# Three of four time norms move from token rows to token columns, with their statistics sent as rows through DRAM; the v mix of the first block waits for the r mix

## The chip, the core and the metric

The kernel runs on one core of one Trainium2 chip. A core has five engines with queues of their own: TensorE (PE, with its weight loads listed as PEld), VectorE (DVE), ScalarE (ACT), GpSimd (POOL) and SyncE (SP, which here only issues transfers). Each engine runs its instructions in the order of its queue; an instruction that waits holds up everything behind it on the same engine. ACT, POOL and SP also issue DMA transfers, and a transfer that waits holds up its queue in the same way. The metric is the device time of one execution in microseconds (us).

## The reference

The input x has 2048 tokens of 512 channels, all float32. The kernel computes an RWKV layer on the layer norm of x, adds x, and then adds a gated feed-forward layer on the layer norm of that sum. Cut to the part that matters here:

```python
xn = layernorm(x)                       # no gain or bias
h  = layer_norm(xn, ln1_g, ln1_b)       # a second norm with gain and bias
hh = time_shift(h)                      # h of the token before
k  = (h*tm_mk + hh*(1-tm_mk)) @ Wk.T
v  = (h*tm_mv + hh*(1-tm_mv)) @ Wv.T
r  = (h*tm_mr + hh*(1-tm_mr)) @ Wr.T
x1 = xn + (sigmoid(r) * wkv(k, v)) @ Wo.T
h2 = layer_norm(x1, ln2_g, ln2_b)       # mixed again, then Wkey, Wval and Wcr
...                                     # then x + that, one more norm, gate, up, down
```

The mean and variance of a norm are taken over the 512 channels of one token. The gain, the bias and the mix factors belong to channels. The matrix products sum over channels.

## The kernel before, in words

The tokens are cut into NB = 4 blocks of TB = 512. Each block has two layouts. With **tokens on partitions**, a tile is 128 tokens by 4 x 512 elements; a mean or a scale is then one number per partition. With **channels on partitions**, a tile holds 4 chunks of 128 channels by 512 tokens; gain, bias and mix factors are then one number per partition, and the products can use the tile as it is. TensorE has to go from the first layout to the second by transposes, 16 of 128x128 for each norm of a block.

The first norm of a block is `time_norm` (L753). It takes the moments of x (`moments`, L396: BATCH_NORM_STATS2 and AGGREGATE, L399 and L400), from them two scales per token (`rsqrt`, L405: for block 1 one GpSimd power at L409, for blocks 2 and 3 three Newton steps on VectorE), scales and centres x into `h` on VectorE (`scaled`, L424, four instructions at L389), and calls `shifted_norm` (L448). That transposes h on TensorE (`transposed`, L436, the matmuls at L441) and lets ScalarE apply gain and bias while it reads PSUM (L453, tile `hT_a`). Block 0 has its own form, `first_block` (L772), with transposes at L810. The residual tile x1 is made on ScalarE from the loaded x and the first of the two scales (L742).

From `hT_a` come three mixed operands, for k, r and v (`mix`, L484): for each chunk of channels one ScalarE multiplication (`shifted`, L494) and one VectorE multiply-add (`mixed`, L393). Where an operand is used by a fast matrix scheme with seven products, four differences (`sums_of`, L462) follow. The second norm, `channel_norm` (L933), has the same shape and fills `hT_b`, from which come the operands `cr` (for `gate_unit`, L951) and `ck` (for `up_unit`, L959). In the second half of the kernel `ffn_in` (L1001) transposes once more.

**What sets the order.** The orders on TensorE, VectorE and ScalarE are fixed by hand: the program is recorded in one pass, and each of those engines keeps the order of recording. The products are laid down one by one (`unit`, L537: seven products; `plain_unit`, L632: the ordinary scheme). After each product of four matmul calls the recorder calls `tick` (L293), which fills an estimated budget of other work (`STEP` = 1.72, charged by `cost`, L204) from queues of generators: `hot`, then `background` (L227 takes the first hot item and the first three background items in turn). `yield 1` in a generator means "let the next item go on"; `need` (L318) forces an item to its end when a product is about to want it. So more VectorE work in one generator moves what comes behind it to later ticks, until `need` forces it. A mix is put into the background by `push_mix` (L862), with a condition: the norm must be finished and an operand tile free.

TensorE has six PSUM banks from one pool (`bank`, L102) and two fixed ones. Weights come by SP through a ring of 12 tiles of 256 KB (`wring`, L77). The tiles of 1 MB for whole blocks of tokens come from a pool of five (`tokp`, L79). GpSimd loads weights, VectorE forms differences of their quarters, and GpSimd stores these to DRAM for later (`prepare`, L144), all through the first half.

Of the kernel before, what the change touches and what calls it, by code (L numbers as in the profile page):

```python
# [9 lines left out]
F32 = mybir.dt.float32  # L10
AF = mybir.ActivationFunctionType
ALU = mybir.AluOpType
# [3 lines left out]
P = 128  # L16
H = 512
NC = H // P
TB = 512
NT = TB // P  # L20
# [9 lines left out]
LN1G, LN1B, LN2G, LN2B, FIRST, MK, MV, MR, CK, CR = range(10)  # L30
NVEC = 10

WK, WV, WR, WO, WCR = range(5)

PLAIN = {(0, WK), (0, WR), (0, WV), (0, WO), (1, WK), (1, WR)}
WKEY = 5
WVAL = 9
# [23 lines left out]
def rwkv_ffn_kernel(  # L61
    ctx: ExitStack,
    tc: tile.TileContext,
    x: bass.AP,
    vecs: bass.AP,
    w: bass.AP,
    wd: bass.AP,
# [2 lines left out]
    nc = tc.nc  # L70
    ntok = x.shape[0]
    NB = ntok // TB
# [12 lines left out]
    dram = ctx.enter_context(tc.tile_pool(name="dram", bufs=1, space=bass.MemoryType.DRAM))  # L85
# [3 lines left out]
    htp = mixes.enter_context(tc.tile_pool(name="htp", bufs=2))  # L89
# [9 lines left out]
    def tok_tile(name):  # L99
        return tokp.tile([P, NT, H], F32, tag="tok", name=name)  # L100
# [103 lines left out]
    def cost(n, fixed=0.135, per=0.00107):  # L204
        spent[0] += max(0.17, fixed + per * n)
# [7 lines left out]
    def flush():  # L213
        while put_off:
            flush_one()
# [27 lines left out]
    finished = set()  # L243
# [68 lines left out]
    def push(name, gen, ready=None):  # L312
        background.append([ready, gen, name, False, background])
# [18 lines left out]
    ident = const.tile([P, P], F32, name="ident")  # L332
# [6 lines left out]
    pt = ps.tile([P, 2, HB], F32, tag="ps", name="warm")  # L339
# [27 lines left out]
    carry = {}  # L367
# [4 lines left out]
    def vcol(row, c):  # L372
        return vec[:, row, c : c + 1]
# [22 lines left out]
    def moments(src, mv):  # L396
        for t in range(src.shape[1]):
            st = small.tile([P, 6], F32, tag="st", name="st")
            nc.vector.bn_stats(st, src[:, t, :])  # L399
            nc.vector.bn_aggr(mv[:, t, :], st)  # L400
            cost(512)
            cost(0)
            yield
# [32 lines left out]
    def transposed(h, evacuate):  # L436
        for c in range(NC):
            pt = bank()
            flat = pt.rearrange("p a b -> p (a b)")
            for t in range(NT):  # L440
                nc.tensor.transpose(  # L441
                    flat[:, t * P : (t + 1) * P], h[:, t, c * P : (c + 1) * P], ident
                )
            evacuate(c, flat)
            spent[0] += 0.4
            yield

    def shifted_norm(s, h, hT, g, b):  # L448
        nc.vector.tensor_copy(hT[:, :, 0:1], carry[s])
        cost(0)  # L450

        def evacuate(c, pt):
            nc.scalar.activation(  # L453
                hT[:, c, 1:], pt, AF.Identity, bias=vcol(b, c), scale=vcol(g, c)
            )

        yield from transposed(h, evacuate)
        yield 1
        nc.vector.tensor_copy(carry[s], hT[:, :, TB : TB + 1])
        cost(0)  # L460
# [11 lines left out]
    def op_free():  # L472
        return live_ops[0] < 3
# [236 lines left out]
    def product_of(b, n, name, sink, by_token, done=None, free=op_done):  # L710
        if (b, name) not in ops:
            flush()
        plain = (b, n) in PLAIN
        B = Lazy((b, name), plain)
# [18 lines left out]
    x1s, ops, hTs = {}, {}, {}  # L733
# [12 lines left out]
    def affine(var, mv):  # L746


        n = mv.shape[1]
        ts(var[:, :n], mv[:, :, 1], EPS, None, ALU.add)  # L750
        ts(var[:, n : 2 * n], mv[:, :, 1], 1.0 + EPS, EPS * EPS, ALU.mult, ALU.add)

    def time_norm(b):  # L753
        xb = xin.pop(b)
        mv = small.tile([P, NT, 2], F32, tag="mv", name="mv")
        yield from moments(xb, mv)
        var = small.tile([P, 2 * NT], F32, tag="var2", name="var2")
        affine(var, mv)
        two = small.tile([P, 2 * NT], F32, tag="two", name="two")
        yield from rsqrt(var, two, 2 * NT, b == 1)  # L760
        rstd, both = two[:, :NT], two[:, NT:]
        h = tok_tile("h")
        yield from scaled(xb, h, mv, both)
        hT = htp.tile([P, NC, TB + 1], F32, tag="hT", name="hT_a")
        hTs[b, "a"] = hT
        tails[b] = residual(b, xb, [(mv[:, t, 0:1], rstd[:, t : t + 1]) for t in range(NT)])
        if b == 1:
            yield 1
        yield 1
        yield from shifted_norm("a", h, hT, LN1G, LN1B)  # L770

    def first_block():  # L772

# [76 lines left out]
    tails = {}  # L850
# [7 lines left out]
    def time_mix(b, name):  # L858
        row, n = {"k": (MK, WK), "r": (MR, WR), "v": (MV, WV)}[name]
        yield from mix((b, name), hTs[b, "a"], row, (b, n) in PLAIN)  # L860

    def push_mix(b, name, gen):  # L862
        norm = f"normb{b}" if name in ("cr", "ck") else f"norm{b}"
        push((b, name, "t"), gen, lambda: norm in finished and op_free())

    qs = {}

# [38 lines left out]
    def v_unit(b):  # L906
# [5 lines left out]
        def done():  # L912
            hidden_sums((b, "g"), q, (b, WO) in PLAIN)

# [367 lines left out]
    for n in "rv":  # L1282
        push_mix(0, n, time_mix(0, n))
# [77 lines left out]
def _layout(inputs):  # L1361

    import numpy as np

    def get(name):
        return np.asarray(inputs["L0_" + name])

    x = np.ascontiguousarray(get("attn_x").reshape(-1, H))
    names = ["ln1_g", "ln1_b", "ln2_g", "ln2_b", "tm_first", "tm_mk", "tm_mv", "tm_mr", "cm_mk", "cm_mr"]
    vecs = np.stack([get("attn_" + n).reshape(NC, P).T for n in names], axis=1)  # L1370

    gu = get("ffn_w_gate_up")
    half = gu.shape[0] // 2
    gate, up = gu[:half], gu[half:]
    key, val, down = get("attn_Wkey"), get("attn_Wval"), get("ffn_w_down")
    blocks = [get("attn_" + n) for n in ("Wk", "Wv", "Wr", "Wo", "Wcr")]
    blocks += [key[j * H : (j + 1) * H] for j in range(4)]
    blocks += [val[:, j * H : (j + 1) * H] for j in range(4)]
    blocks += [gate[j * H : (j + 1) * H] for j in range(4)]
    blocks += [up[j * H : (j + 1) * H] for j in range(4)]  # L1380

    def quarter(m, i, j):
        q = m[i * HB : (i + 1) * HB, j * HB : (j + 1) * HB]

        return q.T.reshape(2, P, HB).transpose(1, 0, 2)

    w = np.stack(
        [
            np.stack([quarter(m, i, j) for i, j in ((0, 0), (0, 1), (1, 1), (1, 0))])
            for m in blocks  # L1390
        ]
    )
    def quarter_quarter(i, j, m, k):
        at = slice(i * HB + m * P, i * HB + (m + 1) * P)
        lo = j * HB + k * P

        q = [down[at, g * H + lo : g * H + lo + P].T for g in range(4)]
        return np.stack(q, axis=1).reshape(P, 4 * P)

    places = ((0, 0), (0, 1), (1, 1), (1, 0))  # L1400
    wd = np.stack(
        [np.stack([quarter_quarter(i, j, m, k) for m, k in places]) for i, j in places]
    )
    return {
        "x": x,
        "vecs": np.ascontiguousarray(vecs),
        "w": np.ascontiguousarray(w),
        "wd": np.ascontiguousarray(wd),
    }
# [19 lines left out]
```

## Time and profile before

| what | value |
|---|---|
| median of 3 runs (lowest to highest) | 1241.83 us (1241.83 to 1243.77) |
| the profiled execution: its time, its span | 1242.04 us, 1239.9 us |
| PE busy | 1231.2 us, 99% |
| DVE busy | 704.8 us, 57% |
| ACT busy | 356.9 us, 29% |
| POOL busy | 153.7 us, 12% |
| transferred | 290.12 MB, mean 234 GB/s |
| transposes L441: for hT_a and hT_b (112), for z (64) | 14.2 us, 7.6 us busy |
| scaling h from x and the two scales (L389, 16) | 8.1 us, 542 ns each |
| hT_a from PSUM (L453, 12) | 8.6 us, 779 ns each |

A line of the groups names the source line, the engine, the operation, the tile written and the tiles read, the shapes, the count, the busy time, the mean duration of one, and the idle time of the engine before them with what ended it. In the timeline a line begins with its start and its length. The chain is read back from the last instruction: at each step to what released it. A matmul call of 128x256 in float32 is two MATMUL records; a transpose is one.

### The profile page before, as it was taken

The page shows a single profiled execution, that of the slowest core. Times are in us where ns is not written, and L with a number is a line of the kernel's source. Part 1 is how long each engine was busy: PE and PEld are TensorE (multiplying, and loading weights), DVE is VectorE, ACT ScalarE, POOL GpSimd, SP SyncE. Part 2 cuts the span into 40 slices and gives each one's busy share as a digit, 9 for nine tenths or more (in the row PEclk, how much of TensorE's full clock was granted, in tenths as well). Part 3 has the DMA queues.
Part 4 walks back from the last instruction along what each step waited for, and adds up shares of the span by engine and source line. Part 5 has one row for each costly group of instructions (what it writes and reads, how often), then busy time and mean ns, then how long its engine had stood idle before and what let it go on. Part 6 is the DMA issues. An engine that isn't in the chain of part 4 may idle for free.

```text
span 1239.9 us, 18124 instructions
## 1 busy us (share of the span) xinstructions
PE 1231.2 (99%) x6552; PEld 1105.0 (89%) x6552; DVE 704.8 (57%) x1307; ACT 356.9 (29%) x661; POOL 153.7 (12%) x278
## 2 busy tenths in 40 slices
PE   8999999999999999999999999999999999999998
PEld 7888888888888888888888888998899888998898
DVE  5877686487763758523542365556546365462466
ACT  5534352142631334212311232122221222112211
POOL 2232221222212222221100000000000000000000
PEclk9999999999999999999999999999999999999999
DMA  6768885898778887899756755895569845785576
GB/s 204 238 216 286 288 277 199 295 318 288 247 255 261 283 261 240 262 329 305 229 145 181 225 144 151 268 339 153 145 183 302 275 141 154 240 295 160 152 223 204
DMA packets 138983, 290.12 MB, mean 234 GB/s; under 512 B 17424, under 2 KB 18576, under 8 KB 137872
## 3 DMA queue, kind: packets, MB, share of 16 engines
q1 hardware_dynamic: 116448, 217.11, 57.4%
q0 software_dynamic: 21440, 70.27, 15.5%
q10 hardware_dynamic: 1008, 1.59, 0.3%
q8 instruction: 53, 0.87, 0.3%
q14 instruction: 34, 0.28, 0.1%
HBM read 246.96 MB, written 41.94 MB: 233 GB/s over the span
## 4 chain that ended last, share of the span: by engine, by line
PE 96%; ACT 1%; DVE 1%; DMA 1%; POOL 0%; issue 0%; DVEq 0%
PE ps L556 54%; PE ps L1160 14%; PE accv L556 11%; PE accx L556 11%; PE ps L658 6%; PE ps L441 1%; DMA raw<-in_wd 1%; ACT mix L494 0%; DMA x<-in_x 0%; ACT mix L823 0%; ACT hT_a L815 0%; DVE mix L393 0%; DVE resid L385 0%; DVE r L385 0%; POOL raw L149 0%
## 5 line engine op out<-in xcount | busy, mean ns | idle before, releaser
L556 PE MATMUL ps<-zT,w 128*128 128x256 f32 x1280 | 289.5, 379 | 0.0
L556 PEld LDWEIGHTS ps<-zT,w 128*128 128x128 f32 x1280 | 241.9, 190 | 32.2
L556 PE MATMUL ps<-mix,w 128*128 128x256 f32 x920 | 210.8, 379 | 0.2 <-ACT u L587 0.2
L556 PEld LDWEIGHTS ps<-mix,w 128*128 128x128 f32 x920 | 174.5, 190 | 24.2 <-ACT u L587 0.6
L385 DVE TENSOR_TENSOR u<-u,accx 128x512 f32<-128x512 f32 x66 | 45.2, 684 | 119.8 <-ACT accx L591 119.8
L1160 PE MATMUL ps<-w,hid 128*128 128x128 f32 x832 | 104.5, 275 | 0.0
L556 PE MATMUL ps<-w,t 128*128 128x256 f32 x456 | 102.3, 379 | 0.0
L1160 PEld LDWEIGHTS ps<-w,hid 128*128 128x128 f32 x832 | 99.8, 192 | 0.8
L556 PEld LDWEIGHTS ps<-w,t 128*128 128x128 f32 x456 | 86.4, 190 | 11.6
L1160 PE MATMUL ps<-w,quads 128*128 128x128 f32 x704 | 89.0, 275 | 0.4 <-ACT r L1172 0.4
L576 ACT COPY accv<-ps 128x512 f32<-128x512 f32 x66 | 37.6, 570 | 179.3 <-PE ps L556 179.3
L1160 PEld LDWEIGHTS ps<-w,quads 128*128 128x128 f32 x704 | 84.2, 192 | 0.9 <-ACT r L1172 0.5
L385 DVE TENSOR_TENSOR raw<-raw 128x512 f32<-128x512 f32 x92 | 63.1, 686 | 37.0 <-DMA raw<-in_wd 11.8
L591 ACT COPY accx<-ps 128x512 f32<-128x512 f32 x66 | 37.7, 571 | 156.9 <-PE ps L556 155.2
L385 DVE TENSOR_TENSOR u<-ps,u 128x512 f32<-128x512 f32 x66 | 45.5, 690 | 55.5 <-PE ps L556 55.2
L658 PE MATMUL ps<-mix,w 128*128 128x256 f32 x320 | 71.0, 380 | 2.1 <-DVE mix L393 2.0
L587 ACT COPY u<-ps 128x512 f32<-128x512 f32 x66 | 38.6, 585 | 112.0 <-PE ps L556 112.0
L1172 ACT COPY r<-ps 128x128 f32<-128x128 f32 x112 | 29.8, 266 | 142.1 <-PE ps L1160 142.1
L1254 POOL DMA_DIRECT2D out<-resid x12 | 8.6, 718 | 498.1 <-DVE resid L385 498.1
L658 PEld LDWEIGHTS ps<-mix,w 128*128 128x128 f32 x320 | 60.2, 190 | 11.0 <-DVE mix L393 3.1
L556 PE MATMUL accv<-zT,w 128*128 128x256 f32 x256 | 60.6, 379 | 0.0
L556 PE MATMUL accx<-zT,w 128*128 128x256 f32 x256 | 60.5, 379 | 0.0
(159 smaller groups left out, 1654.0 us busy)
## 6 DMA issues: line engine op xcount, KB each, us to landing
w<-sum SPq DMA_DIRECT2D x312, 256.0 KB, 3.3
w<-in_w SPq DMA_DIRECT2D x254, 256.0 KB, 3.7
w<-dd SPq DMA_DIRECT2D x112, 256.0 KB, 3.6
raw<-in_w POOLq DMA_DIRECT2D x48, 256.0 KB, 5.5
sum<-raw POOLq DMA_DIRECT2D x48, 256.0 KB, 4.3
w<-d SPq DMA_DIRECT2D x48, 256.0 KB, 3.5
q<-in_w POOLq DMA_DIRECT2D x36, 256.0 KB, 6.0
sum<-q POOLq DMA_DIRECT2D x36, 256.0 KB, 4.0
```

What stands on the lines that cost most here:

```text
L385: nc.vector.tensor_tensor(out, a, b, op)
L441: nc.tensor.transpose(flat[:, t * P : (t + 1) * P], h[:, t, c * P : (c + 1) * P], ident)
L556: mm = nc.tensor.matmul(pz[:, m, :], lhsT=lhsT, rhs=rhs, start=first and g == 0 and m == 0 and k == 0, stop=g == last and k == 1, skip_gro ...
L576: "z", A11, B11, True, pop_held, read=lambda: nc.scalar.copy(accv, acc["z"])
L587: nc.scalar.copy(tmp["u2"], acc["z"])
L591: nc.scalar.copy(accx, acc["z"])
L658: mm = nc.tensor.matmul(acc[i, j][:, m, :], lhsT=act[:, k, lo] if by_token else wg[:, k, lo], rhs=wg[:, k, :] if by_token else act[:, k, : ...
L1160: mm = nc.tensor.matmul(dst, lhsT=x[k][:, g, :], rhs=wt[:, g, :], start=first and g == 0, stop=g == 3, skip_group_check=True,)
L1172: nc.scalar.copy(st["r"][:, m, n * P : (n + 1) * P], st["z"])
L1254: eng.dma_start(out_t[b][:, tokens, cols], rs[b][:, tokens, cols])
```

## The change

**Norm.** For blocks 1 to 3 (`TURNED = 1`) `time_norm` now ends in a new function `turned_norm`. A copy of x with channels on partitions is laid out on the host (`xt`) and loaded as `xT`, 1 MB in one transfer on SP. TensorE transposes only the statistics: four columns of means and four columns of scales, two calls with 4x128 outputs, into one bank. ScalarE copies them to a tile, stores them to DRAM (2 x 512 numbers) and loads each of the two rows back, broadcast to all 128 partitions (256 KB each), all on its own queue. VectorE then subtracts the row of means and multiplies with the row of scales, two TENSOR_TENSOR of 128x512 for each of the four chunks, in place. ScalarE applies gain and bias as before, but from SBUF. The tile `h`, its four scalings and its 16 transposes are gone for these blocks.

**Mix.** In `push_mix` the v mix of block 0 gets one more condition: the r mix of block 0 must be finished, operand differences or not. Before, both began in turn as soon as the norm was done.

```diff
+TURNED = 1
...
         rstd, both = two[:, :NT], two[:, NT:]
+        if b >= TURNED:
+            yield from turned_norm(b, xb, mv, rstd, both)
+            return
         h = tok_tile("h")
...
+    def turned_norm(b, xb, mv, rstd, both):
+        xT = tok_tile("xT")
+        paced(nc.sync.dma_start(xT, xt[b]))
+        yield 1
+        pt = flat(bank())
+        for k, cols in enumerate((mv[:, :, 0], both)):
+            nc.tensor.transpose(pt[:NT, k * P : (k + 1) * P], cols, ident)
+        sb = flat(q_tile("row"))
+        nc.scalar.copy(sb[:NT, : 2 * P], pt[:NT, : 2 * P])
+        nc.scalar.dma_start(
+            stats[b].rearrange("s (t p) -> t s p", p=P),
+            sb[:NT, : 2 * P].rearrange("t (s p) -> t s p", s=2),
+        )
+        for _ in range(3):
+            yield 1
+        rows = []
+        for k in range(2):
+            r = flat(q_tile("row"))
+            nc.scalar.dma_start(r, stats[b][k : k + 1, :].broadcast_to([P, TB]))
+            rows.append(r)
+        tails[b] = residual(b, xb, [(mv[:, t, 0:1], rstd[:, t : t + 1]) for t in range(NT)])
+        hT = htp.tile([P, NC, TB + 1], F32, tag="hT", name="hT_a")
+        hTs[b, "a"] = hT
+        for _ in range(3):
+            yield 1
+        nc.vector.tensor_copy(hT[:, :, 0:1], carry["a"])
+        cost(0)
+        for c in range(NC):
+            tt(xT[:, c, :], xT[:, c, :], rows[0], ALU.subtract)
+            tt(xT[:, c, :], xT[:, c, :], rows[1], ALU.mult)
+            nc.scalar.activation(
+                hT[:, c, 1:], xT[:, c, :], AF.Identity, bias=vcol(LN1B, c), scale=vcol(LN1G, c)
+            )
+            yield
+        yield 1
+        nc.vector.tensor_copy(carry["a"], hT[:, :, TB : TB + 1])
+        cost(0)
...
-        push((b, name, "t"), gen, lambda: norm in finished and op_free())
+        alone = (0, "r") if (b, name) == (0, "v") else norm
+        push((b, name, "t"), gen, lambda: {norm, alone} <= finished and op_free())
...
+    xt = np.ascontiguousarray(x.reshape(-1, TB, NC, P).transpose(0, 3, 2, 1))
```

## The prediction

> **What bounds the kernel now.** I read the page first, then the list of what TensorE waits for, then the chain, then three short stretches of the timeline.
>
> From the page and from TensorE's waits:
>
> ```profile
> PE 1231.2 (99%) x6552; PEld 1105.0 (89%) x6552; DVE 704.8 (57%) x1307; ACT 356.9 (29%) x661; POOL 153.7 (12%) x278
> ...
> PEclk9999999999999999999999999999999999999999
> ```
>
> ```profile
> PE ps L658 <- DVE mix L393: 2.0, 2, 1.1
> PE warm L341 <- POOL ident masks.py:199: 1.4, 1, 1.4
> PE ps L556 <- PE ps L556: 0.4, 1, 0.4
> PE ps L1160 <- ACT r L1172: 0.4, 1, 0.4
> PE ps L556 <- ACT u L587: 0.2, 1, 0.2
> ```
>
> TensorE is the bound from end to end and waits for little (total, times, longest). So a matmul that goes is a gain of its own spacing, and a new wait on TensorE is a loss at its full length. Work on other engines costs only where TensorE comes to wait for it.
>
> The chain gives the price of a transpose (start, length):
>
> ```profile
> 150.88 1.75 PE ps L441 x16
> ```
>
> 16 transposes take 1.75 us, 0.109 us each; a product of eight records beside them takes 1.73, 0.216 each.
>
> Three places of the timeline matter. First, the start of r in block 0, where ScalarE takes four `shifted` in a row, two for r and two for v, ahead of what r needs next:
>
> ```profile
> 23.25 2.54 ACT L494 ACTIVATE mix<-hT_a,onem 128x512 f32<-128x512 f32 x4
> ...
> 27.62 0.75 DVE L393 SCALAR_TENSOR_TENSOR mix<-hT_a,vec,mix 128x512 f32<-128x512 f32 x1 [2.22 <-ACT mix L494]
> ...
> 28.43 5.85 PE L658 MATMUL ps<-mix,w 128*128 128x256 f32 x24 [0.90 <-DVE mix L393]
> ```
>
> Second, the scales of block 1 and the first transposes after them:
>
> ```profile
> 39.82 2.10 POOL L409 TENSOR_TENSOR two<-var,mhalf 128x8 f32<-128x8 f32 x1 [9.18 <-DVE shift L393]
> ...
> 46.20 1.04 PE L441 MATMUL ps<-ident,h 128*128 128x128 f32 x8
> ```
>
> They are known at 41.92, and TensorE wants them only 4.3 us later. Third, the first product of the gate of block 0, which wants `cr`, 0.4 us late already:
>
> ```profile
> 104.95 1.89 PE L556 MATMUL ps<-mix,w 128*128 128x256 f32 x8
> ...
> 105.65 2.55 ACT L494 ACTIVATE mix<-hT_b,onem 128x512 f32<-128x512 f32 x4
> ...
> 106.40 1.42 DVE L393 SCALAR_TENSOR_TENSOR mix<-hT_b,vec,mix 128x512 f32<-128x512 f32 x2
> ...
> 107.25 2.18 PE L556 MATMUL ps<-w,mix 128*128 128x256 f32 x8 [0.41 <-PE ps L556]
> ```
>
> **The parts and their costs.** Beside the trace I use the changed program's order of recording, which fixes the three compute queues.
>
> *Transposes.* Three norms lose 16 each: 48 x 0.109 = -5.25 us, all on the bound. Two calls with 128 columns come back for each: 6 x 0.109 = +0.66. Net -4.6 us.
>
> *First mix.* The order now has r's two `shifted`, then the exponentials, then r's other two. ScalarE is free two `shifted` earlier: the next exponential starts at 24.5 instead of 25.70 (its row in the same stretch), r's third `shifted` ends at 26.4, r's third multiply-add at 27.15 (28.37 before), its fourth at 28.4 (29.63, a row at 28.89 of 0.74). TensorE has r's first two chunks done at 27.53 and before waited 0.90 and, after the third, 0.40 (29.29 to 29.69). Now only about 0.07 stays: -1.23 us. r ends at 39.69 instead of 40.92 (13 chunks of 0.864 after the fourth multiply-add).
>
> *The wait for the scales of block 1.* The two new transposes stand on TensorE's queue right behind r's last product and ahead of all of v. They want `two`, the GpSimd power. VectorE is full up to there (3.86 to 4.00 of each 4 us between 28 and 40) and does the same instructions as before; following its new order with the same durations, it gains only 0.45 us, because v's late third `shifted` makes it wait 0.74. So the power ends at about 41.5, and TensorE, ready at 39.69, waits 1.85 us. Bounds: zero if VectorE gains the full 1.2 us and more, 2.3 us if it gains nothing. I take 1.85; v then starts at 41.7, later than the 40.92 of before, and the second part of the change has bought nothing. Behind the waiting transposes stand v's products, whose readers are VectorE's multiplications; nobody else waits.
>
> *Statistics through DRAM, block 1.* The copy to `row` ends about 42.2 (a copy of 128x128 from PSUM takes 266 ns), the store is issued by 42.65 (0.45 us per issue on ACT, the load of `vec`). Its landing is unknown: 1.6 us as the 64 KB stores at the kernel's end, 5.4 us as the 20 KB load of `vec`, the one small transfer in traffic. ScalarE stands still until then; behind it are one residual activation and the hT_a work, which nobody else needs. Two loads of 256 KB, 0.9 us to issue, 4.5 us to land (such loads on ACT; 6.0 for those on POOL): rows are there between 49.7 and 54.95. The 1 MB of `xT` is issued once SP's last load for k of block 1 is out, 41.21 before; 5.4 to 7.8 us (the 1 MB `resid` loads) put it at 49, so the rows set the start. VectorE reaches its first subtraction at 50.1, does six at 0.60 and then v's third product, which the output product needs at 57.2: free as long as the rows land by 53.0. The late end costs 2.0 us, the early end nothing. I take nothing, since a store is nearer to the stores than to a load in the opening rush. k's mix is then ready at 64.5 and wanted at 69.3.
>
> *The gate of block 0.* VectorE now does eight TENSOR_TENSOR (0.60 back to back) for four scalings (about 0.48): about 3 us more per block. The background work behind it slides, and the order shows where it hurts: before, the 16 transposes of hT_b were spread among v's products, with two products after the last; now all 16 stand together, with one product (1.73) between them and the gate, and all of `cr` is recorded in that last tick. With T the start of the transposes: sg on ScalarE T+0.2, four hT_b 0.70 to 3.5, the accx copy (its product ends at T+3.48) 3.7 to 4.2, two `shifted` to 4.9 and 5.5, two multiply-adds to 5.8 and 6.4. TensorE was ready at T+3.48; its first pair of matmul calls wants the first multiply-add and the next the second, so it loses 2.5 us where it lost 0.86 before (104.95 + 1.73 to the next product at 109.27, less 1.73): +1.7 us. Bounds: 0, if the parts stay spread in time, and 2.5.
>
> *Blocks 2 and 3.* The scales are ready 2.5 us and more ahead of the transposes, rows and xT have four or more products of cover (7 us), and every mix is finished in the order at least 20 us before its product. Nothing on TensorE. VectorE's 3 us more per block lie in stretches with 18.0 to 26.8 of 30 us busy. The 4.6 MB more (three times 1 MB and two rows) meet a weight ring of 12 x 1.73 = 20 us. If that cover is gone, see the rival.
>
> *What a wait may do to the clock.* The trace grants full clock in every slice in spite of waits of 1.06 and 1.37 us, so I charge nothing. The Trainium skill, "TensorE: Matmul & The Clock Gate", section "HAM oscillation — how this bites in real kernels", speaks against a change that adds waits: idle gaps beyond about 3.4 us halve the clock. My two waits stay below that; by the page, each gap that grew past it would cost about 1.7 us more, an estimate from its window of 3.4 us at half rate, and the sum with both would be 1.1 us above before instead of 2.3 below.
>
> **Sum.** -5.25 + 0.66 - 1.23 + 1.85 + 1.7 = -2.3 us against the profiled execution (1242.04, of which 2.1 us lie around the span), which stands 0.2 us above the median. 1241.83 - 2.3 = **1239.6 us**. About 0.2%, 2.5 us, is what a measurement can tell from no change; the forecast lies at that edge.
>
> **Rivals.**
> *The two waits do not come* (the power is early enough, hT_b spreads out in time): -4.6 - 1.2 = -5.8, 1236.0. For it: VectorE often has idle time. Against: both follow from queue order.
> *Slower: the rows of block 1 come late.* Beyond 53.0 each us is a us on TensorE, behind VectorE's in-order wait. Even with before at 55.3, over 0.2% slower from 57.8, which is 15 us after the store's issue, where the slowest rows give 12.3. At that point 1244.3. For it: DMA share 0.88 between 48 and 52. Against: all rows.
> *VectorE's extra work is not covered in blocks 2 and 3*: 26.76 of 30 us are busy between 160 and 190, so up to 3 us on TensorE: 1242.6, no change. Against: VectorE's idle time is mostly waiting for TensorE.
>
> **Chances.** Forecast 0.45, no waits 0.20, VectorE uncovered 0.15, late rows 0.12, the rest 0.08. Its own range for the forecast is 1238.3 to 1241.0. The range 1236.2 to 1243.2 takes in the third rival, and most of the first, and leaves out about 2 in 10. Faster by over 0.2% (below 1239.3): half the forecast and the first rival, 0.43; within 0.2%: 0.40; slower: late rows and some of the rest, 0.17.
>
> **What would show it.** In the changed profile: 64 transposes for hT instead of 112, and six new ones for the statistics; r of block 0 with no wait over 0.1; a TensorE wait of 1 to 2.3 us on POOL's power near 40; one of about 2.5 at the gate near 106, on `cr`; none on rows or xT. I am wrong if TensorE waits on v's or k's operands of block 1 (late rows), or if waits spread over 130 to 400.

## The result, and the profile after

The change makes the kernel slower: 1247.15 us median against 1241.86 for the kernel before, measured side by side. The ratio is 1.0038, with a 95% interval of 1.0028 to 1.0047. The eight executions of the changed kernel lie between 1243.2 and 1249.7 us, those of the kernel before between 1241.8 and 1243.8. So there is something new in the changed kernel that differs from execution to execution. The profiled execution, 1249.7 us with a span of 1247.9, is the slowest of the eight, and shows this most.

From the page of the changed kernel: the busy time of the engines and the granted clock in 40 slices.

```profile
PE 1231.3 (99%) x6510; PEld 1102.8 (88%) x6510; DVE 715.6 (57%) x1319; ACT 358.5 (29%) x664; POOL 154.1 (12%) x278
...
PEclk9999999999999999999999999999999999999999
```

TensorE has 42 matmul records fewer and is busy for the same 1231 us: some matmuls must have become slower, or run at a lower clock. The row of clocks does not show it, because each slice is 31 us wide and 9 stands for everything from 90% on.

What TensorE waits for (total, times, longest), changed kernel:

```profile
PE ps L660 <- DVE e L387: 3.5, 1, 3.5
PE ps L558 <- DVE mix L395: 2.1, 1, 2.1
PE ps L790 <- POOL two L411: 1.4, 1, 1.4
...
PE accv L558 <- ACT accv L578: 1.2, 1, 1.2
...
PE ps L443 <- DVE h L391: 0.5, 1, 0.5
```

Left out are two that were there before, 1.4 us at the start (`warm`) and 1.1 on a mix. These five are new or longer: the output product of block 0 (3.5), the gate of block 0 (2.1), the power (1.4), a copy to `accv` in block 3 (1.2) and transposes of `hT_b` (0.5).

The first part of the timeline of the changed kernel, from r's last products to the output product of block 0 (start, length, engine, line, tile written and tiles read; in brackets how long the engine stood idle before, and on what):

```profile
39.40 0.27 PE L790 MATMUL ps<-ident,mv 128*4 128x128 f32 x1
41.10 0.27 PE L790 MATMUL ps<-ident,two 128*4 128x128 f32 x1 [1.43 <-POOL two L411]
...
43.39 0.51 ACTq L793 DMA_DIRECT2D stats<-row  x1
...
47.26 1.30 ACTq L802 DMA_DIRECT2D row<-stats  x2
...
55.48 0.69 DVE L387 TENSOR_TENSOR xT<-xT,row 128x512 f32<-128x512 f32 x1 [5.79 <-DMA row<-stats]
56.46 3.35 DVE L387 TENSOR_TENSOR xT<-xT,row 128x512 f32<-128x512 f32 x5 [0.28 <-DMA row<-stats]
59.73 0.68 DVE L387 TENSOR_TENSOR e<-ps,e 128x512 f32<-128x512 f32 x1
60.46 15.30 PE L660 MATMUL ps<-w,e 128*128 128x256 f32 x56 [3.55 <-DVE e L387]
```

The store of the statistics is issued at 43.39, the row loads can go out at 47.26, and the second row is there at 56.46. VectorE has stood in front of the first subtraction for 5.8 us, and the multiplication `e` that the output product wants is recorded behind six of them. TensorE waits 3.55 us. The 56 records that follow take 15.30 us; at 0.216 each plus the tail of the last they would take 12.25.

The chain of waits of the changed kernel goes through that row (start, length):

```profile
47.65 8.71 DMA row<-stats
```

At the gate of block 0:

```profile
108.41 1.91 PE L443 MATMUL ps<-ident,h 128*128 128x128 f32 x16
110.15 1.89 PE L558 MATMUL ps<-mix,w 128*128 128x256 f32 x8
...
113.36 2.73 DVE L395 SCALAR_TENSOR_TENSOR mix<-hT_b,vec,mix 128x512 f32<-128x512 f32 x4
114.16 3.68 PE L558 MATMUL ps<-w,mix 128*128 128x256 f32 x8 [2.11 <-DVE mix L395]
```

Sixteen transposes in one heap, one product, then a wait of 2.11 us for `cr`, and eight records that take 3.68 us instead of 1.89.

The clock shows in narrow stretches. Columns: the stretch, its length, busy time (and count) of PE, PEld, DVE, ACT and POOL, the granted clock, the DMA share, GB/s.

```profile
60.00:70.00 10.00, 9.54 (x31) 7.93 (x32) 8.04 (x14) 7.56 (x13) 3.79 (x7) 0.68 0.36 130
...
112.00:114.00 2.00, 0.04 (x1) 0.00 (x0) 1.32 (x3) 1.92 (x4) 1.66 (x4) 1.00 0.46 102
114.00:116.00 2.00, 1.84 (x5) 1.44 (x6) 2.00 (x4) 1.12 (x2) 0.51 (x1) 0.56 0.93 320
116.00:118.00 2.00, 2.00 (x7) 1.62 (x6) 1.93 (x4) 0.12 (x1) 0.00 (x0) 0.58 1.01 389
```

Right behind both long waits TensorE is granted little more than half its clock, as a mean of these stretches. The kernel before has full clock in all such stretches.

**Where the 8.0 us of span went** (1239.9 to 1247.9, profiled executions, by matching TensorE's instructions in both):

| part | us |
|---|---|
| transposes, 48 less, 6 more | -4.6 |
| r earlier and wait for the power, together (v starts at 41.21 instead of 41.02; the two new transposes ahead of it are counted above) | 0.0 |
| wait for the rows of block 1, with the tail of the product ahead of it | +3.7 |
| half clock after it (15.30 - 12.25) | +3.1 |
| gate of block 0: 4.06 lost around its first product, 0.86 before | +3.2 |
| transposes of hT_b of block 1 (0.49 of wait, the rest in their spacing) | +1.4 |
| accv copy in block 3 (1.2 of wait, the rest in the spacing) | +1.4 |
| a wait for a ScalarE copy (`u`) at 487.9 in the kernel before that is gone | -0.5 |
| behind the last product | +0.3 |

Of the 4.06 us at the gate, 2.6 are the wait and the pace at which the mixes of `cr` come (the norms alone and the rows that need not wait, below, have the same order there and full clock behind the wait: 2.61 and 2.60). The half clock is the other 1.4.

### The profile page after: what moved, and what is told of

Its sections match the earlier page's. It is cut to its first block, busy times and chain, and to the rows that moved or that the text cites. A ratio compares the mean times of both kernels' runs of the same rounds, so it can differ in the third digit from the quotient of the medians.

```text
span 1247.9 us, 18079 instructions
## 1 busy us (share of the span) xinstructions
PE 1231.3 (99%) x6510; PEld 1102.8 (88%) x6510; DVE 715.6 (57%) x1319; ACT 358.5 (29%) x664; POOL 154.1 (12%) x278
## 4 chain that ended last, share of the span: by engine, by line
PE 92%; DVE 3%; DMA 3%; ACT 1%; issue 1%; POOL 0%; ACTq 0%; DVEq 0%; POOLq 0%
PE ps L558 52%; PE ps L1212 14%; PE accx L558 11%; PE accv L558 10%; PE ps L660 4%; DMA row<-stats 1%; PE ps L443 1%; DMA raw<-in_w 1%; DVE xT L387 0%; DVE mix L395 0%; DVE st L401 0%; DVE e L395 0%; DMA stats<-row 0%; DMA x<-in_x 0%; DVE raw L387 0%
```

## The experiments

**My theory after the result:** the two transfers in a row bring the rows of block 1 3.5 us too late; the order of recording makes the gate wait 1.25 us more; and waits of about 2 us and more cost about as much again through the clock. **The rival:** the three microseconds more of VectorE work per block are the loss, wherever it shows.

### The change in blocks 2 and 3 alone

```diff
-TURNED = 1
+TURNED = 2
```

> Block 1 keeps the norm of before; only blocks 2 and 3 take the new form, and the first mix is as in the change. Theory A (the loss sits in block 1: its rows come late through DRAM, TensorE waits for them and then runs at half clock, and the gate of block 0 follows on transposes in one heap): the output product of block 0 waits for nothing over 1 us, the gate of block 0 waits at most 0.9 us, the granted clock shows no slice below 0.95 between 40 and 120. Sum: 32 transposes less 4 new ones -3.1, first mix -1.2, and 1.2 to 2.6 back for the late accv wait and the hT_b wait of blocks 2 and 3, so 1238.8 to 1240.5 against 1241.9 for before. Rival B (the three microseconds more of VectorE work per block are the loss, wherever they fall): two thirds of the loss stay, about 1245. If it is below 1241.5, A holds for the place; if it is above 1244, B.

Measured: 1238.09 us (1237.98 to 1238.73), ratio 0.9969 [0.9957, 0.9981]. This is faster than the kernel before. TensorE's waits in it:

```profile
PE ps L660 <- DVE mix L395: 1.1, 1, 1.1
PE accv L558 <- ACT accv L578: 0.5, 1, 0.5
```

The rows, the power and the gate are gone from the list. Two thirds of VectorE's extra work is still there and costs 0.5 us (accv), so the rival falls. Of the -3.9 us, -3.06 are 32 transposes less 4 new ones at 0.109, and -0.8 is the first mix (next run). That these two alone give the whole is partly chance: the profiled execution (1238.73 us) also loses 0.5 at accv and 0.6 at the transposes of hT_b of block 1 (16 of them take 2.36 instead of 1.75), and it gains the 0.5 at 488 us that the table above names. Against the profiled execution of before it is 3.3 us faster.

### The first mix alone

```diff
 # the kernel before
-        push((b, name, "t"), gen, lambda: norm in finished and op_free())
+        alone = (0, "r") if (b, name) == (0, "v") else norm
+        push((b, name, "t"), gen, lambda: {norm, alone} <= finished and op_free())
```

> The kernel before with only the second part of the change: the v mix of block 0 begins when that for r is done. All three norms as before. A: r of block 0 loses its waits of 0.90 and 0.40 us, nothing stands behind it on TensorE that wants the scales of block 1 early, so the 1.2 us reach the end: 1240.6 against 1241.9. Rival: the time turns up again as a wait of v or k of block 0 for mixes that are now later: 1241.9, with a wait of about 1 us on a mix in the first 60 us.

Measured: 1241.13 us, 0.8 less than before; the ratio is 0.9994 [0.9985, 1.0002], so by time alone it is not told from no change. The trace tells more: of the two waits on mixes that add up to 2.0 us before, only the one of 1.1 at the start is left, and there is a new one.

```profile
PE ps L658 <- DVE mix L393: 1.1, 1, 1.1
...
PE ps L441 <- DVE h L389: 0.2, 1, 0.2
```

The waits of 0.90 and 0.40 at r are gone: record by record, v starts 1.2 us earlier than before. But VectorE is not earlier by as much, and the first eight transposes of `h` of block 1 now catch up with its scalings and wait: they begin 1.35 us earlier (44.85 instead of 46.20) and the product behind them 0.96 earlier (46.11 instead of 47.07). So the 1.23 us that I had put down for r are real, and 0.4 of them are lost again 5 us later.

### The norms alone

```diff
-        alone = (0, "r") if (b, name) == (0, "v") else norm
+        alone = norm
```

> The change without its second part: norms of blocks 1 to 3 in the new form, r and v mixes of block 0 in turn as before. A: r ends 1.2 us later, but TensorE's wait for the power of block 1 shrinks by as much (1.43 to about 0.2), v starts at 40.9 to 41.3 as in both, and the rest (rows late, clock, gate) stays: 1246.8 to 1247.5, that is 0 to 0.5 us from the changed kernel. Rival: the earlier r mix is worth its 1.2 us there too: 1248.4.

Measured: 1246.51 us (1245.56 to 1250.22), ratio 1.0042 [1.0028, 1.0056], against 1247.15 with the second part. The wait for the power is 0.70 us instead of 1.43, and v starts at 41.97, later than expected.

```profile
41.86 0.27 PE L790 MATMUL ps<-ident,two 128*4 128x128 f32 x1 [0.70 <-POOL two L411]
41.97 13.98 PE L660 MATMUL ps<-mix,w 128*128 128x256 f32 x64
...
113.96 2.23 PE L558 MATMUL ps<-w,mix 128*128 128x256 f32 x8 [2.11 <-DVE mix L395]
```

In the changed kernel v starts at 41.21, 0.76 us earlier, and 0.25 of that is the earlier opening of its profiled execution. So the second part does bring v forward, by half a microsecond: the power takes 0.7 of the 1.2 that r gains, not all of it. Whether the half reaches the end cannot be told from the times, with four executions here over 4.7 us and eight of the changed kernel over 6.5. The wait for the rows is 4.07 us in this execution, with a clock of 0.66 between 60 and 65. The gate waits 2.1 us again, but behind it the clock is full. The same wait can lower the clock or not.

### Rows that need not wait for the store

```diff
-            nc.scalar.dma_start(r, stats[b][k : k + 1, :].broadcast_to([P, TB]))
+            nc.scalar.dma_start(r, (xt[b][0:1, k, :] if b == 1 else stats[b][k : k + 1, :]).broadcast_to([P, TB]))
```

> The changed kernel, but the two rows of block 1 are loaded, with the same shapes on the same queue, from a row of the transposed input instead of from the statistics, so that the loads need not wait until the store of the statistics has landed; the norm of block 1 is then computed with wrong numbers, all instructions stay. A: the loads are issued near 44 instead of 47.3, land at 50 to 53, VectorE is in time and the output product of block 0 waits for under 0.3 us at full clock: -3.55 -3.05 us, 1240.5 against 1247.15, and the gate's wait may remain. Middle case: they land later than 53 (contention grows as all come together), each microsecond of it stays as a wait: 1242 to 1245. Rival B (VectorE's extra work is the loss): no more than 1 us gained, about 1246.5.

Measured: 1242.65 us (1239.69 to 1244.19), ratio 1.0003 [0.9994, 1.0012], 4.5 us less than the changed kernel: the middle case. The loads go out at 44.2 and the rows arrive at 51.4 and 54.3.

```profile
44.18 2.17 ACTq L802 DMA_DIRECT2D row<-in_xt  x2
...
51.38 0.69 DVE L387 TENSOR_TENSOR xT<-xT,row 128x512 f32<-128x512 f32 x1 [1.48 <-DMA row<-in_xt]
54.30 3.35 DVE L387 TENSOR_TENSOR xT<-xT,row 128x512 f32<-128x512 f32 x5 [2.23 <-DMA row<-in_xt]
...
58.30 3.94 PE L660 MATMUL ps<-w,e 128*128 128x256 f32 x17 [1.18 <-DVE e L387]
```

The second row is 2.16 us earlier than in the changed kernel (56.46) and TensorE's wait is 2.37 shorter. So the price that the prediction gave, one microsecond of TensorE for each microsecond beyond about 53, holds: 54.30 gives 1.18, 56.46 gives 3.55. And the loads alone, without the store ahead of them, are slow there too: the second lands 9.3 us after its issue. The wait of 1.18 leaves the clock full, and so did the gate's wait of 2.1 in this execution:

```profile
108.00:110.00 2.00, 0.95 (x3) 0.58 (x4) 2.00 (x5) 2.00 (x4) 1.41 (x3) 1.00 0.95 242
```

### The waits filled

```diff
+            if n == WO and at == 2:      # ahead of the third product of the output of block 0
+                fill(28)
...
+    def fill(n):
+        pt = bank()
+        for _ in range(n):
+            nc.tensor.transpose(pt[:, 0, 0:P], ident, ident)
...
+        if b == 0:                       # ahead of the gate of block 0
+            need((0, "cr"))
+            fill(16)
```

> The changed kernel with TensorE kept busy through its two long waits: 28 transposes of the identity (28 x 0.109 = 3.1 us) ahead of the third product of the output of block 0, where it waited 3.55 us, and 16 (1.7 us) ahead of the gate of block 0, where it waited 2.1 us. They read nothing that is late and nobody reads them, so the rows and the mixes come no earlier. Theory A (the waits also lower the clock): the remaining waits are about 0.5 us each, the granted clock is 1.0 between 55 and 125, and what the lowered clock cost (3.05 and 1.8 us in the profiled execution of the changed kernel, less in others) is gone: 1243 to 1244.5, with a spread of under 2 us instead of 6.5. If the clock costs nothing: 1247 as before, with the same spread; if the fill itself is on the path: above 1247.

Measured: 1243.81 us (1242.43 to 1245.79, eleven executions), ratio 1.0013 [1.0005, 1.0022]. That is 3.3 us less than the changed kernel, with 44 transposes more and every late operand as late as its loads make it. What is left of the two waits:

```profile
61.28 3.07 PE L660 MATMUL ps<-w,e 128*128 128x256 f32 x13 [1.11 <-DVE e L387]
...
112.00 2.23 PE L558 MATMUL ps<-w,mix 128*128 128x256 f32 x8 [0.33 <-DVE mix L395]
```

The granted clock over a whole execution is 0.997 to 1.000 (0.996 to 0.999 in the changed kernel), and the profiled stretches between 55 and 125 are all at 1.00. The spread is 3.4 us instead of 6.5, though not under 2 as expected. So the wait is only part of what a wait costs; the rest is the clock behind it.

### The transposed x loaded early

```diff
+    def load_xT(b):
+        turned_x[b] = tok_tile("xT")
+        paced(nc.sync.dma_start(turned_x[b], xt[b]))
...
-        xT = tok_tile("xT")
-        paced(nc.sync.dma_start(xT, xt[b]))
+        if b not in turned_x:
+            load_xT(b)
+        xT = turned_x.pop(b)
...
     xin[1] = load_x(1)
+    load_xT(1)
```

> The changed kernel, but the 1 MB of transposed x for block 1 is loaded right behind x of block 1 at the start, and no longer between 40 and 48, just ahead of the rows. Theory 1 (the rows take 8.7 us because they share the DMA engines with that megabyte and the weights): the store lands in 2 to 3 us and the rows in 5 to 6, rows are there by 52 to 53, TensorE's wait at the output product shrinks from 3.55 to under 0.5, and its clock stays up: 1241.5 to 1243. Theory 2 (loading one row of 2 KB to 128 partitions is slow in itself, or the weights alone fill the engines): landing stays at 8 to 9 us, the wait at 3 to 3.5, 1246.5 to 1247.5.

Measured: 1244.00 us (1240.63 to 1248.07), ratio 1.0017 [1.0005, 1.0030], 3.2 us less than the changed kernel. The store has landed by 45.5 (issued at 43.54; 3.8 us in the changed kernel), the first row is there at 50.54, but the second only at 54.42:

```profile
45.49 1.91 ACTq L809 DMA_DIRECT2D row<-stats  x2
...
50.54 0.69 DVE L387 TENSOR_TENSOR xT<-xT,row 128x512 f32<-128x512 f32 x1 [0.70 <-DMA row<-stats]
54.42 3.35 DVE L387 TENSOR_TENSOR xT<-xT,row 128x512 f32<-128x512 f32 x5 [3.19 <-DMA row<-stats]
```

So the megabyte of xT held up the store and the first row (issued at 45.49 and there 5 us later). The other profiled runs agree on the store: 3.8 to 5.5 us to the issue of the rows in the five that load xT of block 1 beside it and wait for it, 1.4 to 2.0 in the three that load it early. The wait at the output product is 1.4 us instead of 3.5; under 0.5 was expected, with the second row 2 us earlier. What slows the second row is not settled by this run. GpSimd issues four loads of 256 KB from 45.28 on, just ahead of it; that they are the cause was not tried.

### The same loads in a quieter place

```diff
+    def probe(b, g):
+        src = stats[3][0:1, :].broadcast_to([P, TB]) if g % 2 else flat(w[g, 0])
+        nc.scalar.dma_start(flat(q_tile("probe")), src)
...
         for g in range(4):
+            probe(b, g)
```

> The changed kernel with 16 loads more in its second half, one before each gate product, all on ScalarE's queue: in turn a plain tile of weights (256 KB, each partition its own 2 KB) and one 2 KB row of the stored statistics, loaded to all 128 partitions (256 KB written). Nobody reads them. Theory 1 (only the traffic makes the rows slow): both land in the same time, 3 to 5 us. Theory 2 (the broadcast is slow in itself): the rows take 6 us and more where the weights beside them take 3 to 4. The time of the kernel is not what is asked here.

Measured: 1247.83 us, one execution. The list of its DMA issues (kilobytes of each, median us from issue to landing):

```profile
probe<-in_w ACTq DMA_DIRECT2D x8, 256.0 KB, 3.5
probe<-stats ACTq DMA_DIRECT2D x8, 256.0 KB, 4.2
row<-stats ACTq DMA_DIRECT2D x6, 256.0 KB, 7.6
```

One row loaded to 128 partitions takes 4.2 us in the second half of the kernel, a plain tile of the same size 3.5. By these medians the broadcast itself costs 0.7 us. The other 3.4 of the 7.6 that the kernel's own rows take come from where they stand: from the traffic there or from the second row being issued right behind the first, which this run does not tell apart.

### Later subtractions in blocks 2 and 3

```diff
 # on top of the change in blocks 2 and 3 alone; ahead of the first subtraction
-        for _ in range(3):
+        for _ in range(5):
             yield 1
```

> Blocks 2 and 3 in the new form, block 1 in the old one, first mix as in the change (1238.09 us), and in addition two more turns of waiting in the order between the loads of the rows and the first subtraction, so that VectorE reaches the subtractions later and holds up less when the rows are late. A: the accv wait of 0.5 us in block 3 goes, nothing else moves: 1237.6. Rival: the mixes or the transposes of the second norm behind it are forced closer to their product and a new wait of 0.5 to 2 us appears: 1238.5 to 1240.

Measured: 1237.54 us, ratio 0.9965 [0.9951, 0.9978]. The accv wait is gone from the list and 0.55 us with it, which the intervals of the two runs alone would not tell apart. In the run before VectorE waited 9.8 us in all for rows of blocks 2 and 3, here not at all, and the 16 transposes of hT_b of block 1 take 1.75 us again. So VectorE stood in front of a row that was still on its way and held up ScalarE's copy behind `hT_a`.

### The order at the gate

```diff
-        slack[0] = max(min(slack[0] + SHARE * length - spent[0], 2.5), -2.5)
+        slack[0] = max(min(slack[0] + SHARE * length * boost[0] - spent[0], 2.5), -2.5)
...
+    boost[0] = 1.2
     k_unit(1)
     push_mix(0, "cr", channel_mix(0, "cr"))
     push_mix(0, "ck", channel_mix(0, "ck"))
     r_unit(1)
     v_unit(1)
+    boost[0] = 1.0
```

> The changed kernel, but between the first product for k of block 1 and the last for v the recorder may lay down a fifth more other work per product, so that the transposes of hT_b of block 0 are spread again (12, one product, 4 or the like, with four products between them and the gate) and the mixes of cr are recorded earlier. The norm of block 1 and its late rows stay. A (the gate's wait comes from the order alone): the 2.1 us wait of the gate goes to under 0.9, and with it the half clock that sometimes follows; the 3.5 us at the output product stays: 1247.15 - 1.25 - about 1, 1244.5 to 1246. Rival (the gate's wait comes from VectorE being behind by its extra 3 us, whatever the order): the wait stays at 1.5 to 2.1, 1246.5 to 1247.5.

Measured: 1243.53 us (1241.04 to 1245.51), ratio 1.0013 [1.0004, 1.0021], 3.6 us less than the changed kernel and more than expected.

```profile
101.28 1.47 PE L444 MATMUL ps<-ident,h 128*128 128x128 f32 x12
102.59 1.89 PE L559 MATMUL accv<-mix,w 128*128 128x256 f32 x8
104.32 0.60 PE L444 MATMUL ps<-ident,h 128*128 128x128 f32 x4
104.76 1.89 PE L559 MATMUL ps<-mix,w 128*128 128x256 f32 x8
...
111.67 1.89 PE L559 MATMUL ps<-w,mix 128*128 128x256 f32 x8
```

With four products between the last transposes and the gate, the gate does not wait at all: -2.1, and no half clock behind it. VectorE does the same work as in the changed kernel, so it was the order. The rows are still late here (a wait of 2.7, and 0.74 of the clock between 60 and 65).

### All of it set right

The changed kernel with xT of block 1 loaded early and the boost of 1.2 at the gate, both as above, and with more turns ahead of the first subtraction, which puts block 1's subtractions behind the last multiplication of v of block 0:

```diff
-        for _ in range(3):
+        for _ in range(7 if b == 1 else 5):
             yield 1
         nc.vector.tensor_copy(hT[:, :, 0:1], carry["a"])
```

> The changed kernel with all that the earlier runs name set right: xT of block 1 loaded at the start, the subtractions of block 1 recorded behind the last product for v of block 0 (four turns later; two turns later in blocks 2 and 3), the gate's order as in the run on the gate. If the account is complete, what is left of the change is 48 transposes less 6 (-4.6), and r's gain together with the wait for the power (+0.3): 1241.9 - 4.3 = 1237.6, with no wait over 1.5 us and full clock. If k of block 1 now waits for its mixes (they are recorded one product ahead), up to 1.5 us more: 1239. Over 1240 the account misses something.

Measured: 1237.01 us (1236.92 to 1237.24), ratio 0.9959 [0.9947, 0.9972]; its waits:

```profile
PE ps L798 <- POOL two L412: 1.4, 1, 1.4
...
PE ps L661 <- DVE mix L396: 1.1, 1, 1.1
PE ps L559 <- DVE mix L396: 0.4, 1, 0.4
```

The account gave 1237.6; the 0.5 us at 488 us that nobody had charged is most of the difference. Three norms in the new form and the first mix, with the same additional VectorE work and the same trip through DRAM, are 4.9 us faster than before once little but the power is waited for, and the five executions lie within 0.3 us.

### Without the wait for the power

```diff
-        yield 1
+        for _ in range(4 if b == 1 else 1):
+            yield 1
         pt = flat(bank())
```

On top of the mended kernel, with `range(4 if b == 1 else 5)` ahead of the subtractions, since the loads now come later by themselves.

> As the mended kernel, but the two transposes of the statistics of block 1 are recorded one product later, behind the first product for v, so that TensorE does not wait 1.4 us for GpSimd's power. All of v and the output product then start 1.4 us earlier, while the rows come when they came. If the rows and mixes keep up: 1.4 us better than the mended kernel, 1236.2. If not, the 1.4 us turn up as a wait at k of block 1 or at the output product: as the mended kernel or up to 1 us slower.

Measured: 1235.44 us, ratio 0.9949 [0.9935, 0.9962], the fastest kernel of the study: 6.5 us below the kernel before. The two transposes stand behind v's first product and no longer wait:

```profile
41.46 0.27 PE L799 MATMUL ps<-ident,two 128*4 128x128 f32 x1
```

The rows kept up. Whether the second part of the change now brings its 1.2 us was not tried: no run has this build without it.

### What a wait does to the clock

```diff
+    STALLS = (3, 9, 6, 12, 15, 4, 10, 7, 13, 18, 5, 11, 8, 14, 6, 9)
+    def stall(n):
+        pt = bank()
+        nc.tensor.transpose(pt[:, 0, 0:P], ident, ident)
+        t = q_tile("stall")
+        for k in range(n):
+            nc.scalar.copy(t[:, 0, 0:P], t[:, 0, 0:P] if k else pt[:, 0, 0:P])
+        nc.tensor.transpose(pt[:, 1, 0:P], t[:, 0, 0:P], ident)
```

> The kernel with blocks 2 and 3 alone in the new form and later subtractions (1237.54 us), with 16 waits of different lengths put on TensorE in its second half, ahead of the gate products: a transpose of the identity, 3 to 18 ScalarE copies of its result in a chain, and a transpose of the copy that nobody reads. Each wait is then about 0.5 us and 0.25 us for each copy, 1.2 to 5 us. If the clock is lowered from a wait of about 2 to 3.5 us on, as the runs so far say (3.5 to 4.1 us: each time; 2.1 us: two times in five; 1.4 us: never), the windows behind waits over 3.5 us show a granted clock of 0.5 to 0.7 for about 3 us, those under 1.5 us full clock, those between some of each. If the lowered clock in the changed kernel came from its place (traffic, VectorE) and not from the wait, all 16 show full clock.

Measured: 1317.47 us, one execution, with 53.3 us of waits. Two waits of the same length, in the timeline:

```profile
717.15 0.33 PE L1138 MATMUL ps<-ident,stall 128*128 128x128 f32 x1 [2.00 <-ACT stall L1137]
1207.81 0.37 PE L1138 MATMUL ps<-ident,stall 128*128 128x128 f32 x1 [2.00 <-ACT stall L1137]
```

All 16, in order of length. "Lost" is one less the granted clock, summed over stretches of 0.5 us for 8 us behind the wait:

| waits of (us) | clock lowered | lost (us) |
|---|---|---|
| 1.68, 1.72 | no | 0 |
| 2.00, 2.33, 2.99, 3.14 | no | 0 |
| 2.00, 2.72, 2.99, 3.32 | yes | 1.71 each |
| 3.65, 3.98 | yes | 1.71, 1.49 |
| 4.37, 5.02, 5.03, 6.33 | yes | 2.67, 2.77, 2.38, 2.13 |

Up to 1.72 us a wait cost only itself, and from 3.65 on each of these cost more. Between them the same length does either, and when it does, the price is 1.71 us.

What decides between two waits of the same length stands in the trace. The clock changes only between full and half, and within each run all its changes lie on one grid of 3.413 us: from the first lowering of this run, at 689.14, each later one and each return is a whole multiple of that away. Here are the two waits in windows of the grid, each with the window behind it:

```profile
713.03:716.44 3.41, 2.12 (x11) 1.56 (x9) 2.05 (x4) 1.73 (x5) 0.00 (x0) 1.00 0.47 148
716.44:719.86 3.42, 2.71 (x13) 2.43 (x14) 1.13 (x2) 1.20 (x5) 0.00 (x0) 1.00 0.17 66
...
1204.55:1207.96 3.41, 1.41 (x8) 0.96 (x7) 1.38 (x2) 1.84 (x7) 0.00 (x0) 1.00 0.45 154
1207.96:1211.38 3.42, 3.42 (x9) 2.71 (x9) 0.00 (x0) 0.00 (x0) 0.00 (x0) 0.50 0.00 0
```

The first wait is cut by the edge at 716.44 into 1.29 and 0.71 us, and the clock stays full. The second lies whole in its window: TensorE is idle for 2.00 of 3.41 us, and the next window runs at half clock. All 16 sort by this number: no window with up to 1.88 us of waiting lowered the clock (the wait of 3.14 was cut into 1.88 and 1.26), and each with 2.00 or more did. The gate's wait of 2.1 us lowered it with 2.11 us in one window (changed kernel) and 1.93 (xT early), and did not with 1.43 (norms alone), 1.77 (rows that need not wait) and 1.95 (same loads in a quieter place). So the boundary lies at 1.9 to 2.0 us within one window, and since the windows begin at other points of the kernel from run to run, the same wait does either. This would also make executions of one kernel differ; that it does is not shown, since one execution of each was traced.

One window at half clock costs 1.71 us. A second one follows where the wait reaches far enough into the first: 0.82 us in the changed kernel were enough, 0.41 in the run of the norms alone were not. That is why the wait for the rows cost 3.1 us in the changed kernel: the clock was at half from 59.64 to 66.47, two windows.

The clock is lowered with no traffic beside it (DMA share 0.00 in the last stretch shown) as well as with it, and not when the waits are filled. So the wait is the cause, not the traffic of its place.

## Why the prediction was wrong, point by point

The forecast was 1239.6 us and faster, and the result is slower by 0.4%, outside the range. By the steps of the prediction:

- *Transposes*: right. -4.6 predicted, -4.6 found: each 16 that went took their 1.75 us with them.
- *First mix*: right at r, in size too. Matched record by record, and less the 0.39 us by which the profiled execution opens earlier, r ends 1.23 us earlier (at 39.40; its old end is 41.02 in the trace, not 40.92). Alone, 0.4 of it is lost again at the transposes of block 1, and the time falls by 0.8.
- *The wait for the scales of block 1*: right in place and mechanism. 1.85 predicted, 1.43 measured (1.6 with the spacing), and VectorE gained the half microsecond it was given (0.45). That the second part buys nothing because of it does not follow, since it was set against the kernel before and not against the norms alone: against those v starts half a microsecond earlier, and the times cannot tell what of that is left at the end. In the last build the wait is gone and 1.6 us came back.
- *Statistics through DRAM, block 1*: **this step failed.** I took 1.6 us for the store and 4.5 for the loads, with upper ends of 5.4 and 6.0. Measured: 3.8, inside its bounds (up to 5.5 in other runs), and 8.7 for the second row, outside them. The store was also issued at 43.39 instead of 42.65. The rule behind it was right: free up to 53.0, then a microsecond each. At 56.46 it gives 3.46, measured 3.55 (although the six subtractions take 0.67 us each and not 0.60). So the mis-sized terms are the two durations, the loads above all. The prediction named the warning (DMA share 0.88 between 48 and 52) and gave it little weight. The change itself puts a megabyte of xT on the engines just ahead of the rows, and the trace of before could not show that; with xT out of the way the store took 1.95 us and the first row 5. The second still took 8.4, and why stays open.
- *The gate of block 0*: right in place, mechanism and size (a loss of 2.5 predicted, 2.6 measured where the clock stays full). With the half clock it is 4.06, which is 3.2 more than before instead of 1.7.
- *Blocks 2 and 3*: nothing was charged; 1.4 us each at accv and at hT_b came in the profiled execution. I had judged by the cover of the rows and left out that an early place in VectorE's order holds up what is recorded behind it. Two turns later took away both, in the kernel with blocks 2 and 3 alone.
- *What a wait may do to the clock*: **this step failed too**, by 4.5 us in the profiled execution (3.1 and 1.4) and by less in others. I charged nothing because waits of 1.06 and 1.37 us left the clock alone, and those are too short to fill 1.9 us of a window. Neither my own wait of 2.5 at the gate nor the rival of late rows was inside what the trace had shown.

The Trainium skill, "TensorE: Matmul & The Clock Gate", section "HAM oscillation — how this bites in real kernels", puts the bound at idle gaps beyond about 3.4 us. Here the measurement decides: a wait of 2.00 us was enough where it lay whole in one window of the clock's grid, and one of 3.14 was not where an edge cut it. The same page, section "The HAM clock gate (the "warmup" mystery)", tells of a window of 4096 cycles that runs freely, 3413 ns at the halved clock. The traces agree on the length, and it is the same while the clock is full: all changes of the clock in a run lie whole multiples of 3.413 us apart. Half of one such window is the 1.71 us that a single lowering cost here.

The rival "Slower: the rows of block 1 come late" is what happened, with the mechanism it named. Its point of decision, rows after 57.8, was too late: they came at 56.5 already, and the clock and the waits of blocks 2 and 3, which it did not count, did the rest. The rival of VectorE's uncovered work was worth up to 2.8 us of the 8.0 (accv and hT_b).

## What to carry to other kernels

Price a new transfer at the place where it will stand, with the transfers that the same change puts beside it; here the durations taken from other places of the kernel were too short by a factor of about two. Where an in-order engine must wait for a transfer, record that work behind everything that the bounding engine wants next: the same change was 5.3 us slower as it stood and 4.9 us faster with its first load of xT earlier, its subtractions later and the gate's order mended. And a wait of about 2 us or more on TensorE is to be counted with a chance of 1.7 us more for the clock, or 3 if it is long: what counts is how much of the wait falls in one of the clock's windows, and a wait of 2 to 3.8 us may or may not be cut by an edge (3.8 is an estimate: two times the 1.9 that a window took without harm). Where a kernel's executions spread more than before, look at the clock in narrow stretches behind the waits.

## What the runs showed of the hardware that was not expected

- The granted clock changes between full and half on a fixed grid of 3.413 us within a run. A window of the grid with 2.00 us or more without a matmul was followed by one at half clock (1.71 us lost), a window with up to 1.88 was not; in between, 1.93 lowered it and 1.95 did not.
- Filling a wait with transposes that nobody reads made the kernel faster by 3.3 us, although they add 4.8 us of work (44 x 0.109) at the place of the wait.
- A store of 4 KB was waited for 3.8 to 5.5 us after its issue with a megabyte of loads beside it and 1.4 to 2.0 without; a 256 KB load of one row to 128 partitions took 4.2 us in a quieter part of the kernel, 8.7 between 47 and 56.
